# Band attention steps: where the next group's query product stands on TensorE

## The chip, the cores and the metric

The kernel runs on one core of a Trainium2 chip. The metric is the device time of one execution in microseconds (us), as the median of three runs. Engines are called as in the profile: PE is TensorE's matrix multiply and PEld its weight load, DVE is VectorE, ACT is ScalarE, POOL is GpSimd, SP is SyncE, which issues the transfers.

## What is computed

One layer over `x` of shape (2, 256, 128, 128): two batches, T = 256 times, 128 frequency bands, 128 channels, float32. It normalizes and attends over time (causal), then over bands (a band mask of width 16), then applies a feed-forward block with an exact GELU; each part adds to `x`.

```python
xt = _ln(x, ln_t_w, ln_t_b).transpose(0, 2, 1, 3)
x = x + _mha(xt, t_wi, t_bi, t_wo, t_bo, H_T, cm).transpose(0, 2, 1, 3)
xf = _ln(x, ln_f_w, ln_f_b)
x = x + _mha(xf, f_wi, f_bi, f_wo, f_bo, H_F, bm)     # bm: |i - j| <= 16
xn = _ln(x, ln_n_w, ln_n_b)
h = jax.nn.gelu(xn @ w1.T + b1, approximate=False)
x = x + (h @ w2.T + b2)
```

`_mha` has four heads of 32 channels: queries, keys and values by one product each, scores, mask, softmax, weighted values, output product.

## The kernel before

Work is cut into groups of four blocks of 128 positions (512 columns). There are 128 groups over time, then 16 runs, each of eight band groups (`OverBands`) followed by the eight feed-forward groups (`FeedForward`) of the same data. `BoundedPath.run` is a software pipeline written out by hand: its loop over `n` calls, for each step, the methods of several groups at different stages. Every instruction is pinned to the order in which it is emitted on its engine, so the order of the calls in the loop is the order on each engine's queue. This document numbers the band steps of a run 0 to 7; in step 7 the next group is a feed-forward group, and in step 0 the group before is one.

In a band step `n` the calls reach the engines so:

- `first_half`, `first_function`, `first_mask` of group n: 64 score matmuls on TensorE into four banks (one per head); VectorE's band mask for the fourth head (`bank<-bank,band`); four exponentials on ScalarE (`pf<-bank`); six selects on GpSimd that mask the other three heads (`pf<-pf`).
- `fetch` of group n + 2: SP fetches its transposed, normalized input (`xnT<-turned`). Then `normalize` and `turn` of group n + 3: VectorE normalizes (`xh`), transposes in blocks (`z`), and SP writes `turned` to DRAM.
- `weigh` of n - 1: sums of the softmax (`bank<-pf,ones`), then weighted values (`bank<-pf,v`). `invert` of n - 1: ScalarE's `ln` and `r`, the reciprocal of the sums.
- `output` and `finish` of n - 2: the output product (`bank<-wn,oT`), and VectorE's addition to the residual (`x<-bank,x`).
- `divide` of n - 1: VectorE's three instructions `bank<-bank,r`, `u<-bank,r`, `oT<-bank,u`.
- `statistics_of_feed(n)`: in some steps the statistics of a feed-forward group on VectorE (`stats`, `mv`), behind `divide`; the root of its variance runs on GpSimd (`rstd`), in steps 4 to 6 at the start of the step, ahead of the masks.
- `queries_keys`, `take_query`, `take_key` of n + 1: both products (`bank<-xnT,wf`, 16 matmuls in all) and ScalarE's copies `qT` and `kT`. Then `values` and `take_values` of n + 1 (`bank<-wf,xnT`, copy `v`).

`product` issues four matmuls of 32 output rows each, one for each column strip of the array; each appears twice in the trace. The eight banks of PSUM are handed out in rotation by `turn_of_bank`: a result takes the bank that comes next, whoever had it eight turns ago. `path.held` lets `weigh` take banks out of the rotation for results that come later: for the outputs (`yp`), and in steps with a following band group for the queries (`qp`) as well; the list is `follow`. In the steady band steps the rotation is four banks of scores, `yp`, `qp`, sums `rp`, `op`, `kp`, `vp`: ten turns a step.

Of the kernel before, what the change touches and what calls it, by code (L numbers as in the profile page):

```python
# [19 lines left out]
P = 128  # L20
# [5 lines left out]
NT = 4  # L26
# [343 lines left out]
class Group:  # L370
# [141 lines left out]
    def queries_keys(self):  # L512
        pass

    def take_query(self):
        pass
# [10 lines left out]
    def weigh(self):  # L527
        pass
# [32 lines left out]
class Attention(Group):  # L561
# [6 lines left out]
            self.dst(), self.src(), self.path.k.orow[self.which].unsqueeze(1).to_broadcast([P, NT, P]), ALU.add  # L568
        )

    def queries_keys(self):
        path = self.path
        wf = path.k.wf[self.which]
        self.qp = path.bank([P, NT * P], "qp", self.place.get("qp", path.held.pop("qp", None)))
        product(path, self.qp, wf[:, 0:P], self.xnT)

        self.kp = path.bank([P, NT * P], "kp", self.place.get("kp"))
        product(path, self.kp, wf[:, P : 2 * P], self.xnT)

    def take_query(self):  # L580
        path = self.path
# [60 lines left out]
def rows_of(h):  # L642
    return slice(h * D, (h + 1) * D)


def product(path, out, weights, x, start=True, stop=True, turn=0):


    for c in range(P // D):
        path.tensor.matmul(out[rows_of(c)], weights[:, rows_of((c + turn) % NT)], x, start=start, stop=stop)  # L650
# [117 lines left out]
class OverBands(Attention):  # L768


    which = 1
    follow = ("yp",)
    by_vector = 1

    def scores(self, heads):
# [38 lines left out]
    def weigh(self):  # L814
        path = self.path

        path.held = {name: path.turn_of_bank() for name in self.follow}
        self.rp = path.bank([P, NT * P], "rp")
        for h in range(H):
            path.tensor.matmul(  # L820
                self.rp[rows_of(h), :], path.k.ones[:, 0:D], self.p[:, h].rearrange("p i q -> p (i q)"),
                start=True, stop=True,
            )
        self.op = path.bank([P, NT * P], "op")
        for i in range(NT):
            c = slice(i * P, (i + 1) * P)
            for h in range(H):
                r = rows_of(h)
                path.tensor.matmul(self.op[r, c], self.v[:, i, r], self.p[:, h, i, :], start=True, stop=True)
# [82 lines left out]
class BoundedPath:  # L912
# [362 lines left out]
    def run(self, x, out):  # L1275
        groups = list(self.groups(x, out))

        def do(n, *names):
            if 0 <= n < len(groups):
                for name in names:  # L1280
                    getattr(groups[n], name)()

        def at(n, kind):
            return 0 <= n < len(groups) and isinstance(groups[n], kind)

        def do_at(n, kind, *names):
            if at(n, kind):
                do(n, *names)


        for i in range(len(groups) - 2):
            if at(i, OverBands) and at(i + 1, OverBands):
                groups[i].follow = ("yp", "qp")

        run0 = [i for i in range(len(groups)) if at(i, OverBands)][: RUN // NT]
        times = range(3 * NT, run0[-1] + 1)
        fours = {i + NT - 1: Four(self, groups[i : i + NT]) for i in times[::NT]}
# [4 lines left out]
        def statistics_of_feed(n):  # L1302
            if n + 5 in early:
                do(n + 5, "statistics")
            if at(n + 4, FeedForward) and n + 4 not in early:
                do(n + 4, "statistics", "root")
# [6 lines left out]
        for n in range(len(groups) + 2):  # L1313
            feeds = [at(n - 2 + i, FeedForward) for i in range(5)]
            bands = [at(n - 2 + i, OverBands) for i in range(5)]
# [79 lines left out]
                fours[n + 2 * NT].refine()  # L1395
            if not bands[2] and not turn:
                statistics_of_feed(n)
            do(n - 1, "weigh")
            do(n - 1, "invert_exactly" if turn else "invert")
            if new is not None:  # L1400
# [21 lines left out]
                if not turn:  # L1422
                    do_at(n + A, OverBands, "statistics", "root")
            do_at(n + 2, OverTime, "queries_keys", "take_query", "take_key")
            do_at(n + 1, OverBands, "queries_keys", "take_query", "take_key")
            if n == run0[0] - 2:
                self.square_keys()
            if n in run0[3:5]:
# [84 lines left out]
```

## Time and profile before

| What | Value |
|---|---|
| median of three runs | 2633.57 us |
| lowest and highest run | 2630.35 and 2633.73 us |
| span of the profiled execution | 2631.9 us |
| TensorE busy | 2617.8 us (99%) |
| VectorE, ScalarE, GpSimd busy | 2140.8, 1838.8, 1958.6 us |
| granted TensorE clock | 1.000 |

The profiled execution is known by its span, from its first to its last instruction; the time of that execution as a run stands in no other place. It lies among the three runs. In the timelines of the profile the columns are the start in us from the span's start, the length of a merged row in us, the engine, the line, the operation, the tiles (out<-in), the shape and the count; brackets at the end tell the idle time ahead of it and who ended it. A row of merged instructions lasts until its last one ends, which overlaps the row behind it; the distance between the starts of two rows is what one took of the engine. All instructions have line 907, that of the helper that pins them.

### The profile page before, as it was taken

The numbers are of one execution on the slowest core, as the hardware profiler recorded it, in microseconds if no ns is written. First come the engines' busy times: TensorE is split into PE (matmuls) and PEld (weight loads), VectorE is DVE, ScalarE is ACT, GpSimd is POOL, SyncE is SP. The second block draws the span as 40 slices with busy tenths as digits, with TensorE's granted clock in tenths as the row PEclk, the third lists the DMA queues.
The fourth block names the chain that finished last, engine by engine and source line by source line (L and its number), as shares of the span: only waits on it lengthen the run. The fifth ranks groups of instructions, "written<-read, shape, count | busy, mean of one in ns | idle before, by whom it ended". The sixth has DMA issues, their size and how long they took to land.

```text
span 2631.9 us, 156460 instructions
## 1 busy us (share of the span) xinstructions
PE 2617.8 (99%) x68688; PEld 1837.4 (70%) x68688; DVE 2140.8 (81%) x6410; ACT 1838.8 (70%) x3543; POOL 1958.6 (74%) x2311
## 2 busy tenths in 40 slices
PE   9999999999999999999999999999999999999999
PEld 6666666666766767666777776667676677777776
DVE  8888888888888887977878779788797797887974
ACT  7989988999899875564655746647557466475573
POOL 7999999999999987666667666665776666757762
PEclk9999999999999999999999999999999999999999
DMA  6656555565565454445454544554454445554543
GB/s 155 167 149 158 149 149 149 155 155 149 149 158 149 122 127 119 115 123 127 118 124 124 123 122 117 126 128 120 122 126 120 120 119 131 123 120 123 123 104 88
DMA packets 469797, 344.97 MB, mean 131 GB/s; under 512 B 43120, under 2 KB 404464, under 8 KB 469104
## 3 DMA queue, kind: packets, MB, share of 16 engines
q1 hardware_dynamic: 468408, 334.41, 50.5%
q8 instruction: 540, 8.85, 1.5%
q14 instruction: 153, 1.25, 0.2%
q10 hardware_dynamic: 696, 0.46, 0.1%
HBM read 167.98 MB, written 166.72 MB: 127 GB/s over the span
## 4 chain that ended last, share of the span: by engine, by line
PE 99%; DVE 0%; issue 0%; DMA 0%; ACT 0%; ACTq 0%; DVEq 0%
PE bank L907 99%; DMA x<-in_x 0%; DVE xh L907 0%; DVE bank L907 0%; DVE res L907 0%; DVE stats L907 0%; DVE oT L907 0%; DVE u L907 0%; DVE xnT L907 0%; ACTq L907 0%; ACT p L907 0%; DVE vy L907 0%; ACT lnv L907 0%; DVE mv L907 0%; ACT root L907 0%
## 5 line engine op out<-in xcount | busy, mean ns | idle before, releaser
L907 ACT ACTIVATE hT<-bank,b 128x512 f32<-128x512 f32 x512 | 348.1, 688 | 524.2 <-PE bank L907 483.2
L907 POOL TENSOR_SCALAR_AFFINE_SELECT pf<-pf 128x512 f32<-128x512 f32 x768 | 477.7, 637 | 185.3 <-ACT pf L907 159.1
L907 PEld LDWEIGHTS bank<-w2T_sb,hT 128*32 128x32 f32 x16384 | 467.4, 110 | 54.8 <-issue 29.0
L907 PE MATMUL bank<-xnT,wf 128*32 128x512 f32 x4096 | 492.4, 592 | 0.5 <-DVE xnT L907 0.5
L907 PE MATMUL bank<-xnT,w1f 128*32 128x512 f32 x4096 | 486.3, 592 | 0.2 <-issue 0.2
L907 PE MATMUL bank<-w2T_sb,hT 128*32 128x128 f32 x16384 | 482.8, 273 | 1.0 <-issue 1.0
L907 ACT ACTIVATE p<-bank 128x512 f32<-128x512 f32 (+1 forms) x1024 | 430.6, 494 | 62.9 <-PE bank L907 62.9
L907 DVE TENSOR_SCALAR xh<-x,mv,rstd 128x160 f32<-128x160 f32 (+1 forms) x1012 | 394.3, 432 | 59.7 <-POOL rstd L907 49.4
L907 POOL TENSOR_SCALAR_AFFINE_SELECT p<-p 128x1024 f32<-128x1024 f32 (+2 forms) x384 | 364.5, 949 | 57.5 <-ACT p L907 49.1
L907 PEld LDWEIGHTS bank<-wf,xnT 128*32 128x32 f32 x8192 | 243.3, 110 | 144.1 <-issue 101.6
L907 POOL TENSOR_TENSOR p<-p,p 128x512 f32<-128x512 f32 x256 | 324.6, 1291 | 10.6
L907 DVE BATCH_NORM_STATS2 stats<-x 128x6 f32<-128x128 f32 x1536 | 329.0, 276 | 3.4 <-DMA x<-in_x 3.4
L907 POOL TENSOR_SCALAR rstd<-mv 128x4 f32<-128x4 f32 x251 | 57.8, 230 | 361.7 <-DVE mv L907 360.5
L907 PEld LDWEIGHTS bank<-xnT,w1f 128*32 128x32 f32 x4096 | 183.6, 110 | 171.6 <-issue 109.6
L907 PE MATMUL bank<-qT,kT 32*64 32x80 f32 (+4 forms) x16384 | 302.0, 271 | 0.1
L907 PEld LDWEIGHTS bank<-qT,kT 32*64 32x64 f32 x16384 | 260.0, 131 | 51.2 <-ACT kT L907 50.6
L907 DVE TENSOR_TENSOR res<-bank,res 128x512 f32<-128x512 f32 (+1 forms) x259 | 170.3, 658 | 153.3 <-PE bank L907 144.7
L907 ACT ACTIVATE pf<-bank 128x512 f32<-128x512 f32 x512 | 265.8, 602 | 35.5 <-PE bank L907 31.3
L907 PE MATMUL bank<-wn,oT 128*32 128x128 f32 x8192 | 283.8, 274 | 0.1
L907 DVE STREAM_TRANSPOSE z<-xh 128x512 f32<-128x512 f32 x380 | 270.3, 711 | 13.3
L907 PE MATMUL bank<-wf,xnT 128*32 128x128 f32 x8192 | 276.5, 273 | 0.0
L907 POOL TENSOR_TENSOR rstd<-rstd,mhalf 128x4 f32<-128x4 f32 x251 | 260.8, 1039 | 20.9
(100 smaller groups left out, 3820.3 us busy)
## 6 DMA issues: line engine op xcount, KB each, us to landing
turned<-z SPq DMA_DIRECT2D x1520, 64.0 KB, 2.7
xnT<-turned SPq DMA_DIRECT2D x380, 256.0 KB, 3.2
x<-res SPq DMA_DIRECT2D x256, 128.0 KB, 2.5
x<-x SPq DMA_DIRECT2D x128, 256.0 KB, 4.1
out<-res SPq DMA_DIRECT2D x252, 128.0 KB, 2.3
x<-in_x SPq DMA_DIRECT2D x124, 256.0 KB, 4.3
x<-in_x SPq DMA_DIRECT2D x4, 128.0 KB, 2.8
x<-in_x SPq DMA_DIRECT2D x6, 64.0 KB, 2.9
```

The source lines that it names most:

```text
L907: return self.tc.keep_in_program_order(emit(*args, **kwargs))
```

## The change

`queries_keys` is split in two. In steps whose group and next group are both band groups, the queries' product of group n + 1 and its copy are issued right ahead of `weigh` of n - 1, that is between the scores of n and the sums of n - 1; keys and values stay behind the outputs. The bank of the queries is taken from the rotation when they are issued, so the steady rotation becomes scores, `qp`, `yp`, `rp`, `op`, `kp`, `vp`, and in step 7 no bank is set aside for queries that do not come. Every instruction stays, with its shape.

```diff
+    def queries(self):
+        path = self.path
+        self.qp = path.bank([P, NT * P], "qp", self.place.get("qp", path.held.pop("qp", None)))
+        product(path, self.qp, path.k.wf[self.which][:, 0:P], self.xnT)
+
+    def keys(self):
         path = self.path
         wf = path.k.wf[self.which]
-        self.qp = path.bank([P, NT * P], "qp", self.place.get("qp", path.held.pop("qp", None)))
-        product(path, self.qp, wf[:, 0:P], self.xnT)
-
         self.kp = path.bank([P, NT * P], "kp", self.place.get("kp"))
         product(path, self.kp, wf[:, P : 2 * P], self.xnT)
+
+    def queries_keys(self):
+        self.queries()
+        self.keys()
...
-        path.held = {name: path.turn_of_bank() for name in self.follow}
+        path.held = {"yp": path.turn_of_bank()}
...
-        for i in range(len(groups) - 2):
-            if at(i, OverBands) and at(i + 1, OverBands):
-                groups[i].follow = ("yp", "qp")
...
+            if bands[2] and bands[3]:
+                do(n + 1, "queries", "take_query")
             do(n - 1, "weigh")
             do(n - 1, "invert_exactly" if turn else "invert")
...
-            do_at(n + 1, OverBands, "queries_keys", "take_query", "take_key")
+            if bands[2] and bands[3]:
+                do(n + 1, "keys", "take_key")
+            else:
+                do_at(n + 1, OverBands, "queries_keys", "take_query", "take_key")
```

More of the change, by code (lines that the diff above doesn't have):

```diff
@@ L569, in bias @@
         )
-    def queries_keys(self):
+    def queries(self):
[3 more added lines that the diff above has]
+    def keys(self):
         path = self.path
         wf = path.k.wf[self.which]
-        self.qp = path.bank([P, NT * P], "qp", self.place.get("qp", path.held.pop("qp", None)))
-        product(path, self.qp, wf[:, 0:P], self.xnT)
         self.kp = path.bank([P, NT * P], "kp", self.place.get("kp"))
         product(path, self.kp, wf[:, P : 2 * P], self.xnT)
+    def queries_keys(self):
+        self.queries()
+        self.keys()
     def take_query(self):
@@ L771 @@
     which = 1
-    follow = ("yp",)
     by_vector = 1
```

## The prediction

> **What bounds the kernel now.** I read the page first. Its first lines say that TensorE is the bound:
>
> ```profile
> span 2631.9 us, 156460 instructions
> ## 1 busy us (share of the span) xinstructions
> PE 2617.8 (99%) x68688; PEld 1837.4 (70%) x68688; DVE 2140.8 (81%) x6410; ACT 1838.8 (70%) x3543; POOL 1958.6 (74%) x2311
> ```
>
> TensorE has 14 us without a matmul in flight, so an order that issues the same matmuls can gain little and can lose wherever a product moves ahead of its operand or its bank. The change concerns only the band steps: 16 runs of eight, numbered 0 to 7 below. Next I read TensorE's timeline in the 13th run and, in the first line, in the 7th. Columns: start, us, engine, line, operation, out<-in, form, count.
>
> ```profile
> 1604.74 1.07 PE L907 MATMUL bank<-pf,ones 128*32 128x512 f32 x8
> ...
> 2226.48 0.97 PE L907 MATMUL bank<-qT,kT 32*64 32x80 f32 x64
> 2227.37 1.06 PE L907 MATMUL bank<-pf,ones 128*32 128x512 f32 x8
> 2228.26 1.06 PE L907 MATMUL bank<-pf,v 128*32 128x128 f32 x32
> 2229.13 1.06 PE L907 MATMUL bank<-wn,oT 128*32 128x128 f32 x32
> 2230.00 1.90 PE L907 MATMUL bank<-xnT,wf 128*32 128x512 f32 x16
> 2231.72 1.06 PE L907 MATMUL bank<-wf,xnT 128*32 128x128 f32 x32
> 2232.71 0.97 PE L907 MATMUL bank<-qT,kT 32*64 32x80 f32 x64
> ...
> 2239.83 1.22 PE L907 MATMUL bank<-pf,ones 128*32 128x512 f32 x8
> ...
> 2246.24 1.34 PE L907 MATMUL bank<-pf,ones 128*32 128x512 f32 x8
> ```
>
> From 2226.48 to 2232.71 stands a whole step (step 4), 6.23 us with no gap: scores 0.89, sums 0.89, weighted values (`op`) 0.87, outputs (`yp`) 0.87, queries with keys 1.72 (0.86 each), values 0.99. The sums of steps 6 and 7, at 2239.83 and 2246.24, take 1.22 and 1.34 instead of 1.06: there something is late. Then VectorE's timeline, from the end of step 1, and through steps 3 and 4:
>
> ```profile
> 2212.93 0.70 DVE L907 TENSOR_TENSOR bank<-bank,r 128x512 f32<-128x512 f32 x1 [0.16 <-ACT r L907]
> 2213.66 0.69 DVE L907 SCALAR_TENSOR_TENSOR u<-bank,r 128x512 f32<-128x512 f32 x1
> ...
> 2221.40 0.70 DVE L907 SCALAR_TENSOR_TENSOR bank<-bank,band 128x512 f32<-128x512 f32 x1 [0.63 <-PE bank L907]
> 2222.01 1.60 DVE L907 TENSOR_SCALAR xh<-x,mv,rstd 128x160 f32<-128x160 f32 x4
> 2223.64 0.71 DVE L907 STREAM_TRANSPOSE z<-xh 128x512 f32<-128x512 f32 x1
> 2224.28 0.65 DVE L907 TENSOR_TENSOR x<-bank,x 128x512 f32<-128x512 f32 x1
> 2224.86 0.69 DVE L907 TENSOR_TENSOR bank<-bank,r 128x512 f32<-128x512 f32 x1
> 2225.58 0.69 DVE L907 SCALAR_TENSOR_TENSOR u<-bank,r 128x512 f32<-128x512 f32 x1
> 2226.31 0.69 DVE L907 TENSOR_TENSOR oT<-bank,u 128x512 f32<-128x512 f32 x1
> 2226.91 0.86 DVE L907 BATCH_NORM_STATS2 stats<-x 128x6 f32<-128x128 f32 x4
> ...
> 2227.97 0.67 DVE L907 SCALAR_TENSOR_TENSOR bank<-bank,band 128x512 f32<-128x512 f32 x1
> ```
>
> VectorE is a second near-bound: in step 3 its instructions stand end to end from 2221.40 to 2227.00, and its whole slack is the 0.63 us in brackets. Where statistics of the feed-forward groups are added (ahead of the masks of steps 4, 5 and 6), the work from band mask to band mask is 2227.97 - 2221.40 = 6.57 us against TensorE's 6.23, so once the slack is gone VectorE falls 0.34 us further behind in each such step. GpSimd waits for those statistics before it masks:
>
> ```profile
> 2241.22 0.23 POOL L907 TENSOR_SCALAR rstd<-mv 128x4 f32<-128x4 f32 x1 [1.27 <-DVE mv L907]
> 2241.53 1.04 POOL L907 TENSOR_TENSOR rstd<-rstd,mhalf 128x4 f32<-128x4 f32 x1
> 2242.54 3.94 POOL L907 TENSOR_SCALAR_AFFINE_SELECT pf<-pf 128x512 f32<-128x512 f32 x6
> ```
>
> The masks of step 6 end at 2242.54 + 3.94 = 2246.48; the sums of step 7, which read them, start at 2246.24. That is the late operand: the chain is VectorE, statistics, root on GpSimd, masks, sums.
>
> **The change, part by part.** No instruction is added or removed. In 112 steps (seven of each run) the queries' product, 8 of the 16 matmuls of a row like that at 2230.00, and its copy move. *TensorE*: the queries take the slot 0.89 to 1.75 after the start of the scores; sums, `op` and `yp` come 0.86 later, up to 4.38; keys and values stay at 4.38 to 6.23. The length stays 6.23. The switch out of the scores, now ahead of the sums, will stand ahead of the queries; I cost it at 0, ends -0.02 to +0.02 a step (scores and sums slots are 0.89 each, an ordinary slot of that size 0.87), so -2 to +2 us in all. *SP and GpSimd*: neither's own order changes; no DMA is moved. *ScalarE*:
>
> ```profile
> 2227.49 2.07 ACT L907 ACTIVATE pf<-bank 128x512 f32<-128x512 f32 x4 [0.29 <-PE bank L907]
> 2229.42 0.63 ACT L907 ACTIVATE ln<-bank 128x512 f32<-128x512 f32 x1
> 2230.08 0.63 ACT L907 ACTIVATE r<-ln 128x512 f32<-128x512 f32 x1
> 2231.11 0.69 ACT L907 ACTIVATE qT<-bank,bq 128x512 f32<-128x512 f32 x1 [0.40 <-PE bank L907]
> 2231.97 0.59 ACT L907 COPY kT<-bank 128x512 f32<-128x512 f32 x1 [0.17 <-PE bank L907]
> ```
>
> The query copy goes from behind `r` to ahead of `ln`, so `ln` and `r` end some 0.6 later (2230.71 becomes about 2231.3, or 4.8 after the scores' start). The key copy stays tied to its product: the copy at 2231.11 starts 0.25 after the end of the queries' slot (2230.00 + 0.86), and the keys' slot ends where it did, so it is costed at 0; ScalarE is free by 4.9, the copy due at 5.49.
>
> *VectorE* is where it costs. `finish` (the row at 2224.28) adds the outputs. Step 3 starts one step before 2226.48, at 2220.25, so `finish` now runs at 4.03, straight behind the transpose, its outputs being ready long before. With outputs ending at 4.38 and the same 0.25 of hand-over it cannot start before 4.63: VectorE sits idle for 0.60 in the middle of the step, and `divide` with all that follows comes 0.60 later. In steps 2 and 3 that uses up the 0.63 of slack, which costs nothing there. But the statistics then start 0.60 later, and so do roots and masks of steps 4 to 6. Four terms come of it, each for one run:
>
> A, step 7. It has no queries to put in between, since the next group is feed-forward. Its sums wait as now, for masks that are late by 0.24 (2246.48 against 2246.24); 0.60 is added, and the corrections B and D below (0.16 more, 0.28 less): 0.72. The wait now is 0.28 (1.34 - 1.06), so it becomes about 0.76: **+0.48**. Ends: 0 (finish is not held) and +0.8 (no catching up through B).
>
> B, step 6. In the new rotation of banks the queries' bank is the one in which the sums of two groups earlier stood (before, the outputs went there). It comes free when the row `u` ends: in step 3 at 2226.27, 6.02 after the start; 0.60 later now, and 0.34 more for each step with statistics: 6.62, 6.96, 7.30, that is 0.39, 0.73 and 1.07 into steps 4, 5 and 6, where it is wanted at 0.89. So 0.18 in step 6, plus about 0.1 of hand-over (scores begin 0.15 after the key copy's end, 2232.71 against 2232.56; I take between 0 and that): **+0.28**, ends 0 and 0.6 (were the hand-over and the lag each twice that). What waits behind these matmuls is all of TensorE's queue.
>
> C, step 2. There `divide` of the step before waits for `r` (0.16 in brackets), which is now 0.6 later: `u` ends at 2214.35 + 0.60 = 2214.95, and the queries' slot starts at 2214.91 (2227.37, the end of the scores two steps on, less 12.46): **+0.1**, ends 0 and 0.2.
>
> D, steps 4 to 6. Sums come 0.86 later there, the masks 0.60: the wait of step 6 (1.22 - 1.06) goes: **-0.16**. Ends -0.16 and 0.
>
> Sum 0.70 a run, 11.2 us for 16. Where TensorE is held by something else in steps 4 to 6, VectorE catches up and A and B shrink; I take 2 us off for that: +9.
>
> E, the transposed input `xnT`. It is fetched by SP in the step before; the queries read it 2.6 us earlier than before (from 3.52 to 0.89).
>
> ```profile
> 1603.18 0.34 SPq L907 DMA_DIRECT2D xnT<-turned  x1
> ```
>
> ```profile
> DMA to landing us min/median/max: 2.6/3.0/4.9
> ```
>
> The second line is that of tile `xnT` over the second two thirds of the span. The first is the fetch for step 6 of the 7th run. With the median it lands at 1606.18; the old use is hidden, but the new one is wanted where the sums' row stands, at 1604.74: 1.4 us late. That is the worst but one; reading the fetches of steps 2 to 6 of all 16 runs in the same way, nine of 80 are late, by 0.1 to 1.7 us, most of them in two runs, where one wait serves the next: 4 to 7 us in all, I take **+5**. Ends: 0 (they land at 2.6 and are hidden by VectorE's lateness) and +20 (many land towards 4.9). The Trainium skill, page "DMA: Bandwidth & Descriptors", section on the anatomy of one DMA, gives 2.0 us plus bytes over 436 GB/s, there fitted for another issue path; for 256 KB an estimate by that page is 2.6 us. By it E would be about 3 and the sum 2 us lower; the trace has that as its minimum, and its median is higher, so the median is used.
>
> Sum: 9 + 5 = +14, on the span of 2631.9: 2646. The median of the runs, 2633.57, stands 1.7 above that span, so the forecast is **2648**.
>
> **The rivals.** *Faster, by the scores' wait for keys.* The list of waits has
>
> ```profile
> PEld bank L907 <- ACT kT L907: 50.6, 255, 0.2
> ```
>
> and the values' slot, 0.99, is 0.12 longer than the equal work of `op`. If scores wait there for a key copy that the query copy holds back, moving the query copy away would give 0.12 x 112 = 13 us: 2620. It decides if the key copy can start 0.1 sooner. Against it: that copy waits for its own product (0.17 in brackets), not for ScalarE, and a delay of 0.2 in all 255 blocks, the time steps too, looks like a cost of switching tile shapes. 8 in 100.
>
> *No change that can be measured.* If `finish` hands over sooner or the 0.63 of slack carries into step 4, A falls to 0, B and C vanish, D stays: -3 with E of 5: 2635. For it: the slack is as large as the delay. Against: the statistics stand behind `divide` with no slack between. 20 in 100.
>
> *Transfers bind.* A fetch wait holds TensorE's queue, thereby scores, masks, the next transpose and the next fetch. With landings between median and 4.9, E is 20 rather than 5: 2663. For it: the fetch has margins of under 2 us in most steps; against: most land before they are wanted. 12 in 100.
>
> The forecast has 60 in 100. For it: every handicap is read off rows of quiet stretches; against: A rests on one delay carried through three steps, which any pause of TensorE shortens.
>
> **How the numbers follow.** A change under 0.2% (5.3 us, somewhat over the 3.4 that three runs spread) cannot be told from none. Slower: 59 of the forecast's 60 and the transfers' 12: 0.71. Same: the 1 left and 18 of the quiet case's 20: 0.19. Faster: the keys' 8 and the quiet case's other 2, where E is 0 as well: 0.10. The range goes from 2635, the quiet case, to 2664, the transfers'; about 15 in 100 lie outside. The forecast's own range is 2640 to 2656: E between 0 and 10, the sum of a run between 0.5 and 0.9.
>
> **What would show it.** In the changed profile: `finish` on VectorE about 4.6 after the scores' start with a wait on TensorE's bank of about 0.6 in steps 2 and 3 (now none); sums of step 7 longer, towards 1.9; sums of step 6 back to 1.06; a gap ahead of the queries in step 6 of undisturbed runs; query copies with the long wait gone; and a few gaps of around 1 us ahead of queries whose fetch was late. The prediction is wrong if `finish` still follows the transpose without a wait, if step 7 keeps its 1.34, or if the values' slot shrinks to 0.87.

## The result, and the profile after

The changed kernel takes 2648.56 us (median; 2646.45 to 2648.94) against 2632.49 (2630.35 to 2633.73) for the kernel before, now the median of five runs: a ratio of 1.0058, 95% interval 1.0047 to 1.0069. It is slower by 0.6%. The forecast was 2648. Two runs of the experiments, one of 2717.26 us (the changed kernel with `finish` free) and one of 5417.56 us (the kernel before), were far slower than the others of their kernel and are left out of all times and ratios below. The first lines of the page after:

```profile
span 2647.1 us, 156393 instructions
...
PE 2614.3 (99%) x68688; PEld 1793.1 (68%) x68688; DVE 2142.6 (81%) x6410; ACT 1835.4 (69%) x3543; POOL 1955.9 (74%) x2311
```

The span is 15.2 us longer (2631.9 before), while the busy times of the four computing engines (weight loads apart) are the same to within 4 us: what was added is waiting. The list of TensorE's waits says for what, over the second two thirds of the span (line, tile and releaser; then us in total, times, longest). Before, that list held one row:

```profile
PE bank L907 <- issue: 2.7, 7, 0.8
```

After, it begins so:

```profile
PE bank L912 <- DVE oT L912: 14.5, 17, 1.1
PE bank L912 <- DMA xnT<-turned: 2.4, 5, 0.9
PE bank L912 <- DVE stats L912: 1.8, 2, 1.3
PE bank L912 <- DVE mv L912: 1.5, 1, 1.5
```

The largest part, 14.5 us, are 17 waits of up to 1.1 for one instruction of VectorE, `oT`. TensorE's timeline shows where. The first line shows queries that wait for a late fetch, in step 5 of the 8th run; then come step 3 of the 9th run and its steps 6 and 7.

```profile
1709.52 1.06 PE L912 MATMUL bank<-xnT,wf 128*32 128x512 f32 x8 [1.55 <-DVE mv L912]
...
1802.18 0.97 PE L912 MATMUL bank<-qT,kT 32*64 32x80 f32 x64
1803.08 1.07 PE L912 MATMUL bank<-xnT,wf 128*32 128x512 f32 x8
...
1820.87 0.97 PE L912 MATMUL bank<-qT,kT 32*64 32x80 f32 x64
1821.98 1.06 PE L912 MATMUL bank<-xnT,wf 128*32 128x512 f32 x8
1822.86 1.04 PE L912 MATMUL bank<-pf,ones 128*32 128x512 f32 x8
...
1826.32 1.06 PE L912 MATMUL bank<-wf,xnT 128*32 128x128 f32 x32
1827.31 0.97 PE L912 MATMUL bank<-qT,kT 32*64 32x80 f32 x64
1829.34 1.07 PE L912 MATMUL bank<-pf,ones 128*32 128x512 f32 x8 [1.06 <-DVE oT L912]
```

The first row names VectorE's `mv`, but its fetch was issued at 1705.35, and tile `xnT` in that stretch has

```profile
DMA to landing us min/median/max: 4.0/4.0/4.0
```

so that it landed at about 1709.4, 0.1 before the queries. In step 3 queries follow scores after 0.90; in step 6 after 1.11, so 0.21 is lost. In step 7 the sums start 2.03 after the scores instead of 0.90: 1.13 lost, with `oT` as releaser. VectorE in the same 9th run, in step 3, then `u` in step 6 and `oT` in step 7:

```profile
1805.51 0.71 DVE L912 STREAM_TRANSPOSE z<-xh 128x512 f32<-128x512 f32 x1
1806.82 0.69 DVE L912 TENSOR_TENSOR x<-bank,x 128x512 f32<-128x512 f32 x1 [0.59 <-PE bank L912]
1807.42 0.69 DVE L912 TENSOR_TENSOR bank<-bank,r 128x512 f32<-128x512 f32 x1
...
1821.23 0.69 DVE L912 SCALAR_TENSOR_TENSOR u<-bank,r 128x512 f32<-128x512 f32 x1
...
1828.50 0.69 DVE L912 TENSOR_TENSOR oT<-bank,u 128x512 f32<-128x512 f32 x1
```

`finish` (at 1806.82) waits 0.59 for the outputs and starts 4.64 after the scores. `u` ends at 1821.92, and the queries of step 6 start 0.06 later: its bank is what they waited for. `oT` ends at 1829.19, and the sums of step 7 start 0.15 later.

The length of each step is the distance between the starts of two score rows. Summed over the 16 runs (15 for step 7, whose length reaches through the feed-forward groups to the next run's first scores), in us:

| Steps | Before | After | Difference | Predicted |
|---|---|---|---|---|
| 0 and 1 | 202.9 | 202.0 | -0.9 | 0 |
| 2 | 99.9 | 101.8 | +1.9 | C 1.6 |
| 3 to 5 | 303.7 | 305.8 | +2.1 | most of E (5) |
| 6 | 101.8 | 103.2 | +1.4 | B and D 1.9 |
| 7 | 928.6 | 939.7 | +11.1 | A 7.7 (16 runs), less 2 for catching up |
| all | 1636.9 | 1652.5 | +15.6 | 14 |

The total was met, but step 7 cost about one and a half times what A had given it. Its size is what the first experiments are about.

### The profile page after: what moved, and what is told of

It reads as the page before. It is cut to its first block, busy times and chain, and to the rows that moved or that the text cites. A ratio compares the mean times of both kernels' runs of the same rounds, so it can differ in the third digit from the quotient of the medians.

```text
span 2647.1 us, 156393 instructions
## 1 busy us (share of the span) xinstructions
PE 2614.3 (99%) x68688; PEld 1793.1 (68%) x68688; DVE 2142.6 (81%) x6410; ACT 1835.4 (69%) x3543; POOL 1955.9 (74%) x2311
## 4 chain that ended last, share of the span: by engine, by line
PE 85%; DVE 13%; DMA 1%; issue 1%; SPq 0%; ACT 0%; POOL 0%; ACTq 0%; DVEq 0%
PE bank L912 85%; DVE xh L912 2%; DVE bank L912 2%; DVE u L912 2%; DVE oT L912 2%; DVE x L912 1%; DVE stats L912 1%; DVE z L912 1%; DMA xnT<-turned 1%; DVE mv L912 0%; SPq L912 0%; DMA turned<-z 0%; DMA x<-in_x 0%; ACT pf L912 0%; DVE res L912 0%
## 5 line engine op out<-in xcount | busy, mean ns | idle before, releaser
L912 PE MATMUL bank<-xnT,wf 128*32 128x512 f32 x4096 | 514.2, 595 | 8.5 <-DMA xnT<-turned 2.4
L912 PEld LDWEIGHTS bank<-w2T_sb,hT 128*32 128x32 f32 x16384 | 459.9, 110 | 69.5 <-issue 48.5
L912 PE MATMUL bank<-xnT,w1f 128*32 128x512 f32 x4096 | 475.2, 592 | 0.0
L912 PE MATMUL bank<-w2T_sb,hT 128*32 128x128 f32 x16384 | 474.9, 273 | 0.0
L912 PEld LDWEIGHTS bank<-xnT,w1f 128*32 128x32 f32 x4096 | 156.2, 110 | 189.0 <-issue 164.6
L912 PE MATMUL bank<-wn,oT 128*32 128x128 f32 x8192 | 277.7, 274 | 0.3 <-issue 0.2
```

The lines of the kernel that those rows point to most:

```text
L912: return self.tc.keep_in_program_order(emit(*args, **kwargs))
```

## The experiments

The theory for A: in steps 2 to 6 the changed rotation is scores (four banks), `qp`, `yp`, `rp`, `op`, `kp`, `vp`. In step 7 the turn of `qp` drops out, so the sums get the bank that held `op` in step 6, which VectorE reads last, with `oT`. Before, a `qp` turn was set aside in step 7 too and stayed unused, so that the sums got a bank that had long been free. The rival: the sums wait for GpSimd's masks, as predicted, and the bank comes free at about the same time by chance. Each kernel was timed beside the kernel before, whose median in the three sets was 2630.74, 2630.55 and 2632.18, so the ratios are what is compared. All of them, with the lengths of steps 2, 6 and 7 as most of the 16 runs have them (without any loss they would be 6.23, 6.23 and 61.71 us):

| Kernel | Time | Ratio (95% interval) | Step 2 | Step 6 | Step 7 |
|---|---|---|---|---|---|
| before | 2632.49 | 1 | 6.23 | 6.39 | 61.94 |
| after | 2648.56 | 1.0058 (1.0047 to 1.0069) | 6.29 | 6.44 | 62.76 |
| after, one spare turn | 2643.95 | 1.0048 (1.0034 to 1.0062) | 6.29 | 6.44 | 62.51 |
| after, root late | 2649.05 | 1.0068 (1.0054 to 1.0082) | 6.29 | 6.44 | 62.76 |
| after, both | 2643.45 | 1.0049 (1.0036 to 1.0063) | 6.29 | 6.44 | 62.35 |
| before, root late | 2628.34 | 0.9989 (0.9980 to 0.9998) | 6.23 | 6.23 | 61.93 |
| after, `finish` free | 2640.60 | 1.0036 (1.0023 to 1.0049) | 6.29 | 6.23 | 62.58 |
| the same, late copy | 2638.22 | 1.0026 (1.0016 to 1.0035) | 6.23 | 6.23 | 62.28 |
| after, fetch earlier | 2644.73 | 1.0050 (1.0037 to 1.0063) | 6.29 | 6.45 | 62.76 |
| before, root late, statistics spread | 2627.18 | 0.9986 (0.9977 to 0.9995) | 6.23 | 6.23 | 61.71 |
| after, all holds removed | 2628.73 | 0.9985 (0.9976 to 0.9994) | 6.23 | 6.23 | 61.85 |

**One spare turn.** The changed kernel, with one bank turn in step 7 that nobody uses:

```diff
         path.held = {"yp": path.turn_of_bank()}
+        if self.spare:       # the last band group but one of a run
+            path.turn_of_bank()
```

> The changed kernel, with one bank turned over unused in step 7 between the outputs' bank and the sums' bank, as the kernel before did. In the changed kernel the sums of step 7 wait 1.13 us (scores' start to sums 2.03 in place of 0.90); VectorE's oT, which frees the bank eight turns back, ends at 1829.19, the masks of step 6 at 1829.05, the sums start at 1829.34. Theory (bank first, masks close behind it): with the spare turn the sums take the key product's bank, long free, and wait for the masks alone: they start about 0.25 us earlier, in about 13 of 16 runs; 3 to 4 us less, about 2645 against 2648.5. Rival (masks alone, as the prediction had it): nothing changes, the sums still start 2.03 after the scores.

Step 7 shrinks by 0.25, 62.76 to 62.51, and `oT` no longer holds the sums. TensorE's timeline in step 7 of the 4th run, with one row of its weight loads (every matmul and every weight load has two records):

```profile
1289.84 0.97 PE L915 MATMUL bank<-qT,kT 32*64 32x80 f32 x64
1290.74 1.52 PE L915 MATMUL bank<-pf,ones 128*32 128x512 f32 x6
1291.65 0.63 PE L915 MATMUL bank<-pf,v 128*32 128x128 f32 x8
1292.09 0.60 PE L915 MATMUL bank<-pf,ones 128*32 128x512 f32 x2
```

```profile
1291.63 0.11 PEld L915 LDWEIGHTS bank<-pf,ones 128*32 128x32 f32 x2 [0.75 <-POOL pf L915]
```

The sums start at once, 0.90 after the scores, but only two of the four heads' run on. The weight load for the third head's comes 0.89 later, at 1291.63, and names GpSimd's masks (`pf`) as releaser; the second records of the last two heads' sums start at 1292.09. So the bank was the last claimant, by 0.25, and the masks stand right behind it with 0.80 (62.51 - 61.71). The bank theory holds; the masks' 0.80 is close to the 0.76 that the prediction gave them.

**Root late.** The changed kernel, with GpSimd's root of the feed-forward variance behind the masks instead of ahead of them:

```diff
-            if n + 4 in early:
-                do(n + 4, "root")
             do(n, "first_half", "first_function", "first_mask")
+            if n + 4 in early:
+                do(n + 4, "root")
```

> The changed kernel, with GpSimd's root of the feed-forward variance (steps 4 to 6) moved behind the masks of its step, so that no mask waits for VectorE's statistics. Theory (bank first): the masks of step 6 end about 1.5 us sooner, but the sums of step 7 still wait for VectorE's oT: 2.03 after the scores' start, time unchanged within 1 us of 2648.5. Rival (masks alone): the wait of 1.13 us in step 7 goes, 13 runs of 16: about 2634.

Nothing changed in step 7: 62.76 in both. GpSimd and TensorE, in the same run as above:

```profile
1290.02 1.04 POOL L912 TENSOR_TENSOR rstd<-rstd,mhalf 128x4 f32<-128x4 f32 x1
1292.25 3.93 POOL L912 TENSOR_SCALAR_AFFINE_SELECT pf<-pf 128x512 f32<-128x512 f32 x6 [1.19 <-ACT pf L912]
```

```profile
1290.57 0.97 PE L912 MATMUL bank<-qT,kT 32*64 32x80 f32 x64
1292.59 1.07 PE L912 MATMUL bank<-pf,ones 128*32 128x512 f32 x8 [1.06 <-DVE oT L912]
```

The masks for the sums of step 7 are now done before the root (1290.02), and the next ones, at 1292.25, wait 1.19 for their exponentials. With the masks early the sums still start 2.02 after the scores, with the same releaser. The rival, masks alone, falls.

**Both.** The spare turn and the late root together.

> Both of the last two edits: sums of step 7 with a free bank and with early masks. Theory (two holds, bank and masks, one behind the other): the whole wait of 1.13 us goes: 13 to 15 us less than the changed kernel, about 2634; what is left over the kernel before is late fetches and the waits of steps 2 and 6 (together some 8 us), less the mask waits of the kernel before (some 5 us). Rival (the wait in step 7 has another cause, such as VectorE's lateness through another operand): a wait of 0.3 us or more stays in step 7.

This was a miss of my theory: step 7 went to 62.35, and the time to 2643.45 and not 2634. As the rival had it, more than 0.3 stays, through another operand. TensorE from step 7 into the second feed-forward step:

```profile
1289.55 0.96 PE L915 MATMUL bank<-qT,kT 32*64 32x80 f32 x64
1290.44 1.07 PE L915 MATMUL bank<-pf,ones 128*32 128x512 f32 x8
...
1304.32 1.90 PE L915 MATMUL bank<-xnT,w1f 128*32 128x512 f32 x16
1306.73 1.08 PE L915 MATMUL bank<-wn,oT 128*32 128x128 f32 x32 [0.51 <-DVE oT L915]
```

```profile
1299.47 1.61 DVE L915 TENSOR_SCALAR xh<-x,mv,rstd 128x160 f32<-128x160 f32 x4 [1.48 <-POOL rstd L915]
...
1306.25 0.43 DVE L915 TENSOR_SCALAR oT<-u 128x512 f32<-128x512 f32 x1
```

The sums of step 7 wait for nothing (0.89). But 16 us later the outputs of the last band group start 2.41 after the row ahead of them, where such a row of 16 takes 1.72 of the engine elsewhere: 0.69 lost, and VectorE's `oT` of that group ends at 1306.68, 0.05 before. On the way there VectorE waits 1.48 for GpSimd's root of its own statistics; that wait is 1.48 in the kernel before and in the changed kernel too (1300.73 and 1837.49), so it passes the lateness on and does not make it. VectorE is late, and three consumers stand in a row: the bank first (1.13), the masks behind it (0.80), the outputs behind those (0.64, from 62.35 - 61.71). Whoever is removed, the next collects.

**The same root, in the kernel before.** The edit of the second experiment on the kernel before the change.

> The kernel before, with the root moved behind the masks. Theory (masks late in steps 6 and 7 of the kernel before, by 0.16 and 0.28): both waits go; 3 to 6 us less than the kernel before, about 2628. Rival (those waits belong to something else): unchanged, 2632.

```profile
1287.20 0.97 PE L907 MATMUL bank<-qT,kT 32*64 32x80 f32 x64
1288.09 1.07 PE L907 MATMUL bank<-pf,ones 128*32 128x512 f32 x8
...
1301.97 1.90 PE L907 MATMUL bank<-xnT,w1f 128*32 128x512 f32 x16
1303.97 1.08 PE L907 MATMUL bank<-wn,oT 128*32 128x128 f32 x32
```

```profile
1303.49 0.43 DVE L907 TENSOR_SCALAR oT<-u 128x512 f32<-128x512 f32 x1
```

The 0.16 of step 6 is gone, as masks were its cause. The wait ahead of the sums of step 7 is gone too (0.89), yet step 7 keeps its 61.93: the outputs now start 2.00 after their predecessor instead of 1.72, and VectorE's `oT` ends 0.05 before them, at 1303.92. The time falls by 2.4 us (2630.74 to 2628.34), a little less than the 3 to 6 expected. So the kernel before has the same debt, 0.2 a run, and the prediction's reading of it, late masks, named only the first that collects.

**Where the lateness comes from.** In the changed kernel, `finish` of n - 2 adds the bank of the group behind it (`op` of n - 1), which is ready earlier, so that it does not wait for the outputs:

```diff
-                do(n - 2, "output", "finish")
+                do(n - 2, "output")
+                groups[n - 2].yp = groups[n - 1].op.rearrange("p (a b) -> p a b", a=NT)
+                do(n - 2, "finish")
```

> The changed kernel, but in band steps whose two groups behind are band groups VectorE's finish adds the weighted values of group n - 1 (complete about 0.6 us before finish is due) in place of the outputs of group n - 2, so that it does not wait for TensorE: that part of the result is left out. Theory (the hold of finish by 0.6 us makes VectorE late, and all waits of steps 6 and 7 follow): finish follows the transpose at 4.0; divide now waits for ScalarE's r (4.83) in place of finish, 0.4 earlier than in the changed kernel; the wait of step 6 goes, that of step 7 falls from 1.13 to about 0.9: 5 to 6 us less, 2643 against 2648.5. Rival (lateness comes from ScalarE's order, r, not from finish): unchanged, 2648.

```profile
1804.17 0.71 DVE L912 STREAM_TRANSPOSE z<-xh 128x512 f32<-128x512 f32 x1
1804.81 0.65 DVE L912 TENSOR_TENSOR x<-bank,x 128x512 f32<-128x512 f32 x1
1805.68 0.70 DVE L912 TENSOR_TENSOR bank<-bank,r 128x512 f32<-128x512 f32 x1 [0.22 <-ACT r L912]
```

VectorE in step 3: `finish` follows the transpose with no wait, but `divide`, next on the queue, now waits 0.22 for ScalarE's `r`, which the query copy ahead of it made late. Step 6 is at 6.23; step 7 gains 0.18 (62.58). The next experiment takes that second hold away too: the query copy goes behind `r`.

```diff
-                do(n + 1, "queries", "take_query")
+                do(n + 1, "queries")
             do(n - 1, "weigh")
             do(n - 1, "invert_exactly" if turn else "invert")
+            if bands[2] and bands[3]:
+                do(n + 1, "take_query")
```

> As the last one, and the copy of the queries put back behind r on ScalarE, with the product still early. The same part of the result is left out. Theory (both holds of VectorE are then gone): divide at 4.6 as in the kernel before; step 2 at 6.23 in place of 6.29; step 7 waits about 0.5 for the bank that oT frees (1.3 + 0.15 against 0.9), in place of 1.13: 11 us less than the changed kernel, about 2637. What is left over the kernel before, some 6 us, is that bank and the late fetches. Rival (finish and copy explain only a part): 2642 or more.

```profile
1803.98 0.71 DVE L912 STREAM_TRANSPOSE z<-xh 128x512 f32<-128x512 f32 x1
1804.61 0.65 DVE L912 TENSOR_TENSOR x<-bank,x 128x512 f32<-128x512 f32 x1
1805.19 0.69 DVE L912 TENSOR_TENSOR bank<-bank,r 128x512 f32<-128x512 f32 x1
```

No wait is left in VectorE's step 3. Step 2 loses its 0.06, so C was `divide` waiting for `r`, as predicted; step 7 falls to 62.28. The two largest waits of TensorE in this kernel, against 14.5 for `oT` in the changed kernel:

```profile
PE bank L912 <- DMA xnT<-turned: 5.9, 5, 2.2
PE bank L912 <- DVE oT L912: 4.6, 8, 0.7
```

With `finish` and `r` free, the waits for `oT` are a third of what they were in all. Part of that is VectorE catching up behind the longer waits for fetches: in most runs step 7 is still 0.57 above 61.71, against 1.05 in the changed kernel, so about half is gone there. So the order of the queries makes VectorE late by way of two instructions; what remains is the rest of VectorE's debt, some of which the kernel before has too, and the late fetches, larger here than in the changed kernel.

**The fetch.** In the changed kernel, SP's fetch for group n + 2 reads the data of the group before it, which has been in DRAM for a step longer; it no longer waits for the transposed block of its own group.

```diff
+            if at(n + 1, OverBands) and at(n + 2, OverBands):
+                groups[n + 2].turned = groups[n + 1].own
             do_at(n + 2, (OverBands, FeedForward), "fetch")
```

> The changed kernel, but in the band steps SP fetches the transposed input of the group one earlier, which landed a step ago, so that no query waits for a late landing: the attention over bands then works on other data. Theory (late fetches cost about 6 us in the changed kernel: gaps of 0.2 to 1.6 us ahead of queries in some eight steps): those gaps go; where they had let VectorE catch up, step 7 takes back up to half: 3 to 6 us less, about 2644. Rival (those gaps come from the fetch of instructions, or transfers are hidden): unchanged, 2648.

```profile
PE bank L912 <- DVE oT L912: 14.6, 16, 1.1
PE bank L912 <- issue: 0.8, 2, 0.4
PE bank L912 <- DMA xnT<-turned: 0.7, 2, 0.5
```

The waits put down to the fetch fall from 2.4 to 0.7, and with them go the two rows `stats` and `mv` (1.8 and 1.5), whose gaps stand ahead of queries too: 5.7 to 0.7 in all. The medians differ by 3.8 (2648.56 and 2644.73), of which the kernel before, 1.9 faster in that set, makes up half: by the ratios, 1.0058 and 1.0050, it is 2.1, less than their intervals tell apart. The steps in the two traces, summed as in the table above, differ by 3.1, at the lower end of the 3 to 6 expected. The wait for `oT` stays as it was.

**All holds removed.** The changed kernel with the spare turn, the late root, the free `finish`, the late copy and the early fetch.

> The changed kernel with its queries' product still early, and every hold found so far taken away at once: finish adds the weighted values of group n - 1 (the outputs are left out of the result there), the query copy stands behind r, the fetch reads the group one earlier (the attention over bands then works on other data), step 7 turns over a spare bank, and the root stands behind the masks. Theory (the place of the queries' product costs nothing by itself; all of the 16 us came through these holds): steps 2 to 6 at 6.23, step 7 to the next run at 61.7 to 61.95, 2627 to 2631, no slower than the kernel before and about as fast as that kernel with the late root (2628.3). Rival (the early product itself costs TensorE time, by switching out of the scores or by an operand not yet named): 2634 or more, with a step longer than 6.23 in most runs.

The ratio is 0.9985, as for the kernel before with the late root (0.9989). Steps 2 to 6 stand at 6.23, and the waits of TensorE (second two thirds) are down to these:

```profile
PE bank L915 <- issue: 1.3, 3, 0.8
PE bank L915 <- DVE u L915: 0.2, 1, 0.2
PE bank L915 <- ACT kT L915: 0.2, 1, 0.2
PE bank L915 <- DMA xnT<-turned: 0.2, 1, 0.2
```

Step 7, at 61.85, keeps 0.14: in the 4th run the outputs of the last band group start 1.91 after the row ahead of them (1304.50 and 1306.41), so VectorE is still a little late. The early queries by themselves cost TensorE nothing that could be measured. The loss of 16 us came through these holds together; since one hides behind another, the runs give no share of each.

**A version for use.** If VectorE's debt is the matter, the kernel before has some of it too. Beside the late root, the statistics of the first two feed-forward groups were moved a step earlier; they stand in steps 2, 3 and 5 instead of 3, 4 and 5:

```diff
-            if n + 5 in early:
+            if n + 6 in early and at(n + 4, OverBands):
+                do(n + 6, "statistics")
+            if n + 5 in early and not at(n + 3, OverBands):
                 do(n + 5, "statistics")
```

> The kernel before with GpSimd's root behind the masks, and the statistics of the first two feed-forward groups one step earlier (behind divide of steps 2 and 3, the third stays behind that of step 5), so that VectorE has a quiet step between. Theory (VectorE's lateness adds up to 0.94 us over three steps in a row and is paid at the first consumer, 0.23 in most runs of the kernel with the late root): with lateness of at most 0.65 that is worked off in step 4 and again in step 6, the 0.23 goes: 61.71 from step 7 to the next run: 3 to 4 us less than with the late root alone, 2624 to 2625. Rival (those 0.23 are not VectorE's): unchanged, 2628.

Step 7 is at 61.71 in most runs, so the debt is gone. The time, 2627.18, is 0.14% under that of the kernel before and the lowest of all; it was expected at 2624 to 2625, and its lead over the late root alone (0.9989) lies within the intervals. Over the second two thirds of its span TensorE's list of waits has one row left:

```profile
PE bank L907 <- issue: 1.3, 4, 0.4
```

## Why the prediction was right, point by point

- **The hold of `finish`**: right. Predicted start 4.63 after the scores, with a wait of 0.60; the rows show 4.64 and 0.59. That VectorE's slack of 0.63 is used up by it, and that what comes later is passed on, is what the free `finish` and the late copy showed together.
- **A, step 7**: the mechanism was incomplete and the term mis-sized. Predicted +0.48 (a wait of 0.76 instead of 0.28, for masks); measured +0.82 in the length of the step, a wait of 1.13, for a bank. The failed step is "Its sums wait as now, for masks". Masks alone would have made 0.80. The prediction worked out the bank turns for steps with queries (B) and not for the one step where the turn of the queries drops out, though the diff shows it.
- **B, step 6**: right in place and cause, `u` of VectorE and the queries' bank: 0.21 against 0.28, because the hand-over took 0.06 and not 0.1, and the lateness was smaller.
- **C, step 2**: 0.06 against 0.1, through `r`, as told. **D**: the sums of step 6 are back at 1.04, as told.
- **E, the fetch**: predicted +5; 5.7 us of waits in the trace, 5.0 of which went with an earlier fetch, but only 2 to 4 us of the time. A pause of TensorE lets VectorE catch up: step 7 of the 8th run, behind the late fetch quoted above, has 62.33 instead of 62.76, and so have the 7th and 12th, each behind a pause in step 5. The landings of tile `xnT` after, over the second two thirds:

```profile
DMA to landing us min/median/max: 2.6/3.0/5.2
```

  The median is as before, and most transfers land before they are wanted. The Trainium skill, page "DMA: Bandwidth & Descriptors", section on the anatomy of one DMA, gives 2.0 us plus bytes over 436 GB/s, fitted there for transfers that GpSimd issues; for 256 KB an estimate by that page is 2.6 us. The trace agrees with it in the shortest landing only, and the waits come from the longer ones.
- **The total** came out within 1 us, partly by luck. Against the five runs of the kernel before the loss is 16.1, and the sum was 14. A was too small by 3 to 5 us (11.1 against 7.7, or 5.7 with the catching up), and most of that was made up by B with D (1.4 against 1.9), C (0.06 x 16 = 1.0 against 1.6), E (3.0 of the lengths of steps 2 to 5 against 5), and 0.9 that steps 0 and 1 gave back, which the sum did not have.
- **The rivals**: the scores' wait for keys fell, since the values' slot stays 0.99 (1826.32 to 1827.31). The key copy, tied to its own product, still ends 0.16 before the next scores (1808.25 and 1808.41), so whether the 0.12 in that slot is a wait for it or a switch of tile shape stays open. No change fell: `finish` did wait, and `u` ended 1.05 into step 6, close to the 1.07 that the lateness carried through steps 4 to 6 had given. Late transfers were there, at 2 to 4 us of the time against the 20 of that rival.

## What to carry to other kernels

On an engine that is the bound, a product moved ahead of its neighbours costs by what it displaces: here the outputs came 0.86 later, and with them the work of a second engine that had 0.63 of slack. Lateness of such an engine is a debt that the first consumer in line collects; removing that wait alone shows only the next consumer, so look for what makes it late, and spread its load. When an order with rotating buffers changes, work out who had each buffer before for the irregular steps above all, where a turn drops out.

## What the runs had not led me to expect

- With the spare turn, a wait for one head's masks stands in the middle of the sums: those of two heads run, and the third head's start 0.89 after the first (1290.74 and 1291.63). The fourth head, which VectorE masks, stands behind it on the queue and starts no sooner. Though half of the sums run on time, the step loses 0.80.
- The hand-over from the end of a VectorE instruction to a waiting matmul was 0.05 to 0.15 us in the rows above, against the 0.25 from a product's slot to ScalarE that the prediction used.
- Waits with no releaser ("issue") stand in the lists of nine of the eleven kernels over the second two thirds, 0.4 to 3.7 us in all and up to 1.1 each; no experiment here was aimed at them, and their cause is open.
